# ScalarE's activation tables in a two-layer kernel: one load after every function, or a load where the written order needs one

## The chip, the cores and the metric

The kernel runs on one core of a Trainium2 chip. The metric is the device time of one execution in microseconds (us). A core has five engines that run beside each other and wait for one another by semaphores: TensorE (PE in the profile; its weight loads are PEld), VectorE (DVE), ScalarE (ACT), GpSimd (POOL) and SyncE (SP), which here only issues DMA transfers. All data is float32.

## The reference

The input x is two images of 48 x 48 positions with 768 channels. Two layers are applied, each as x + f(groupnorm(x)).

```python
# layer 0: attention of 12 heads, each position over the 7 x 7 positions around it
qkv = gn(x) @ w_qkv
scores = einsum('nhije,nhiajbe->nhijab', q * 64 ** -0.5, k_near)
o = einsum('nhijab,nhiajbe->nhije', softmax(scores), v_near)
x = x + o @ w_out
# layer 1: a selective scan over the 2304 positions, forwards and backwards, 1536 channels
xz = einsum('bld,ed->bel', gn(x), in_proj_w)
def branch(x, z):                       # once as it stands, once reversed, own parameters
    x = silu(dwconv(x, conv_w, conv_b))           # 4 taps
    dt, Bm, Cm = split(einsum('bdl,ed->bel', x, x_proj_w))
    delta = softplus(dt_proj_w @ dt + dt_proj_b)
    h = exp(delta * A) * h + (delta * x) * Bm     # for each of 16 states, along l
    y = sum over states of h * Cm, + x * Dp
    return y * silu(z)
x = x + einsum('bdl,cd->blc', forward + backward, out_proj_w)
```

Four functions need a table of ScalarE: exp (in softmax and in the scan), ln (in the group norm), silu and softplus.

## The kernel before, in words

**Tiling.** Positions lie along the free dimension in chunks of 384 (`CHUNKS`, six per image), channels on the 128 partitions in 12 blocks. Attention works on six row bands per image. The scan stage runs over units: image, direction, chunk, channel block, 2 x 2 x 6 x 12 = 288 units in this order. The states of a channel block are taken in four groups of four.

**One unit of the scan** (`scan`). For each group g: the input product hb = (delta x) * B, 128 x 1544 (L1225), on DVE from the PSUM tile `du` or on POOL from the tile `u`; ACT writes exp(delta A) for one state at a time, 128 x 384, into the PSUM tiles `da0` and `da1` (L1247), two states in each; DVE scans two states at once (L1258, `tensor_tensor_scan`) in place in `hb`; POOL multiplies by C (L1273); PE adds the 16 states up by transposes into `py` (L1290); ACT copies `py` to `yt` (L1316). ACT also copies `u` to `du` (L1202), the chunk's borders into `bc` (L1231) and the last state to `state` (L1281).

**Every third unit** (`deltas_of`). PE makes the pre-activation of delta for three channel blocks (L1151), ACT copies it into `dlt` (L1157) and takes softplus of 128 x 1152 at once (L1162), then ACT makes x * Dp (`vt`, L1170) and POOL makes delta x (L1175). That is 96 softplus.

**Beside the scan** (`in_proj`). For the next chunks PE makes x and z (L382), ACT does the convolution's first tap from PSUM into `uz` (L928), DVE the three others (L935), ACT copies z (L955), and `finish` takes silu (L961) of a whole `uz` tile, 128 x 2304, and stores it. The first chunk of image 0 goes before any scan: there six tiles of 128 x 1536 (named bc0 to bc7, borrowed buffers) are made, each followed by silu. That is 74 silu in all. Attention of image 1, the projections to delta, B and C (`x_proj`) and the output projections also run beside the scan.

**What sets the order.** All work is registered with `add`: an engine, an estimated duration in ns, a function that issues the instructions, and a key that says when it is wanted. `Order.run` (L153) then plays the program through with these estimates and writes out one order for all engines; each engine executes its instructions in this order. For each engine it picks among the works that are ready the one of smallest rank:

```python
over = max(0.0, t + x.ns - soon - self.DUE) / 2
rank = (max(t + over, free[e] + 150.0), x.first)
```

`t` is when the work could start, `soon` the earliest time at which a work marked `due` (the scan's exps) could start, DUE is 100 ns, and `over` counts only for works ahead of the oldest main key. Some input products have an `alt`: the planner may put them on DVE or on POOL. Where it sees TensorE idle long, it adds filler transposes (L1491).

**Tables.** The table that has exp and ln is loaded at the start (L263). The compiler places a load in front of each silu and softplus, and the kernel itself issues a load back directly after each (L962, L1163). The planner's estimate for both functions includes 2600 ns for the two loads.

Of the kernel before, what the change touches and what calls it, by code (L numbers as in the profile page):

```python
# [45 lines left out]
KB = 3  # L46
EARLY = 20
# [40 lines left out]
class Work:  # L88


    __slots__ = ("eng", "ns", "fn", "key", "job", "bufs", "waits", "then", "ready", "tail", "size", "first", "alt", "due", "opens")


class Order:
# [19 lines left out]
            for p in (parts,) if isinstance(parts, int) else parts:  # L114
                yield buf, p

    def add(self, eng, ns, fn, key, r=(), w=(), job=False, size=0, after=None, early=0, alt=None, due=False, opens=None):
        x = Work()
        x.eng, x.ns, x.fn, x.key, x.job, x.size = eng, ns, fn, key, job, size
        x.then, x.ready, x.tail, x.first = [], 0.0, self.TAIL[eng], key - early  # L120

        x.alt = alt

        x.due = due

        x.opens = opens
        before, bufs = set(), {}
        for buf, p in self.cells(r):
            c = (buf, p)
            bufs[buf] = None  # L130
            if c in self.wrote:
                before.add(self.wrote[c])
            self.read.setdefault(c, []).append(x)
        for buf, p in self.cells(w):
            c = (buf, p)
            bufs[buf] = None
            if c in self.wrote:
                before.add(self.wrote[c])
            before.update(self.read.pop(c, ()))
            self.wrote[c] = x  # L140
        before.discard(x)
        if after is not None:
            before.add(after)
        x.waits = len(before)
        for y in before:
            y.then.append(x)
        x.bufs = [b for b in bufs if b.pool is not None]
        for b in x.bufs:
            b.left += 1
        self.works.append(x)  # L150
        return x

    def run(self):  # L153
        free = dict.fromkeys(self.TAIL, 0.0)
        ready = {e: [] for e in free}
        slots, dma = {}, 0.0
        mains = sorted((x.key for x in self.works if not x.job), reverse=True)
        done_keys = {}
        for x in self.works:
            if not x.waits:  # L160
                ready[x.eng].append(x)
                assert not x.alt
        out = []
        left = len(self.works)
        extra, spare = 0.0, False
        while left:
            while mains and done_keys.get(mains[-1], 0):
                done_keys[mains[-1]] -= 1
                mains.pop()
            horizon = (mains[-1] if mains else 1e9) + self.LOOK + extra  # L170
            best = None
            for e, works in ready.items():
                pick = None
                soon = min((max(free[e], x.ready) for x in works if x.due), default=1e12)
                for x in works:
                    if x.key > horizon:
                        continue
                    t, more = max(free[e], x.ready), {}
                    for b in x.bufs:
                        if not b.end:  # L180
                            had = slots.get((b.pool, b.tag), ())
                            n = more[b.tag] = more.get(b.tag, 0) + 1
                            if len(had) + n > b.bufs:
                                old = had[n - 1 - b.bufs]
                                if old.left:
                                    t = None
                                    break
                                t = max(t, old.end + self.SEM)
                    if t is None:
                        continue  # L190
                    over = 0.0
                    if mains and x.key > mains[-1] < self.last and not x.due:
                        over = max(0.0, t + x.ns - soon - self.DUE) / 2
                    rank = (max(t + over, free[e] + 150.0), x.first)
                    if pick is None or rank < pick[0]:
                        pick = rank, t, x
                if pick and (best is None or pick[1] < best[0]):
                    best = pick[1], pick[2], e
            if not best:

                extra += 1.0
                assert extra < 400, "the plan is stuck"
                continue
            extra = 0.0
            t, x, e = best
            ready[x.eng].remove(x)
            gap = t - free["PE"]
            if e == "PE" and spare and gap > self.GAP:
                y = Work()
                y.eng, y.ns, y.key, y.job, y.size = e, 0.8 * (gap - 300.0), x.key, True, 0  # L210
                y.then, y.bufs, y.due, y.fn = [], [], False, lambda y=y: self.idle(y.ns)
                out.append((free[e], y))
            if x.opens is not None:
                spare = x.opens
            if x.alt:
                ready[x.alt[0]].remove(x)
                if e != x.eng:
                    x.eng, x.ns = x.alt
            for b in x.bufs:
                if not b.end:  # L220
                    slots.setdefault((b.pool, b.tag), []).append(b)
            free[x.eng] = t + x.ns
            if x.eng == "SP":
                dma = max(dma, t + 500.0) + x.size / 290.0
                end = max(dma, t + x.ns) + 2100.0
            else:
                end = t + x.ns + x.tail
            for b in x.bufs:
                b.left -= 1
                b.end = max(b.end, end)  # L230
            for y in x.then:
                y.waits -= 1
                y.ready = max(y.ready, end + self.SEM * (y.eng != x.eng))
                if not y.waits:
                    ready[y.eng].append(y)
                    if y.alt:
                        ready[y.alt[0]].append(y)
            if not x.job:
                done_keys[x.key] = done_keys.get(x.key, 0) + 1
            out.append((t, x))  # L240
            left -= 1
        return out
# [3 lines left out]
def tile_kernel(  # L246
# [3 lines left out]
    nc = tc.nc  # L250
# [74 lines left out]
    order = Order()  # L325
    marks = {"n": 0}
    pars = []

    def add(eng, ns, fn, key, r=(), w=(), job=False, size=0, after=None, early=0, alt=None, due=False, opens=None):

        news = [x[0] if isinstance(x, tuple) else x for x in w]

        def issue():
            for v in news:
                if v.ap is None:
                    v.ap = v.pool.tile(v.shape, F32, tag=v.tag, name=v.name, bufs=v.bufs)
            fn()

        if eng == "PE":

            ns *= 1.04 if key < 0 else 1.05
        return order.add(eng, ns, issue, key, r, w, job, size, after, early, alt, due, opens)

    def mm(n, cl):
        return n * (cl * 1.69 + 5)
# [1 line left out]
    def act(n, pointers=0):  # L347
        return 60 + 90 * pointers + n * 0.833
# [45 lines left out]
    def parameters(key):  # L394

        for i, (conv_w, conv_b, xpT, dtT, dt_b, A_log, Dp) in enumerate((fwd, bwd)):
# [15 lines left out]

            v = Buf(f"par{i}", ap=True)
            add("SP", 5000, fetch, key + i, w=[v], job=True)
            add("ACT", 800, decay, key + i + 0.5, r=[v], w=[v], job=True)
            pars.append(v)
        for j, t in enumerate(xd[0] + xd[1]):

# [8 lines left out]
    def group_norm(stats, n, key, job):  # L427
# [62 lines left out]
        for i, (eng, ns, fn, r, w) in enumerate((  # L490
# [10 lines left out]
            ("PE", 600, spread, [g, gT], [acc]),  # L501
            ("DVE", 200, last, [acc, mean], [rstd, shift]),
        )):
            add(eng, ns, fn, key + 0.01 * i, r, w, job=job)
        return shift, rstd

    def stats_of(b, key, job, tags):
# [21 lines left out]
    def attention(b, start, end, job, T):  # L529
# [228 lines left out]
        def heads(n, p, i, u, kc, ks, qs, vs, vat, mask, to, key):  # L758
# [16 lines left out]
            for j in range(2):  # L775
# [8 lines left out]
                def exponentials(j=j):  # L784
# [5 lines left out]
                add("DVE", dve(NKEY), masked, key, r=[sc[j], mask], w=[pr[j], (sm, j)], **S)  # L790
                add(
                    "ACT", act(NKEY, 1) + 90, exponentials, key, r=[pr[j], (sm, j)],
                    w=[pr[j], (sm, 2 + j)], **S,
                )

                if j or not job:
# [83 lines left out]
    def in_proj(b, i, start, end, conv=True, gate=True, nk=KB, tags=("uz",), banks=("mm",), proj=None):  # L880
# [78 lines left out]
        def finish(k0, nk, uz, dsts, key):  # L959
            def silu():  # L960
                nc.scalar.activation(uz[:, :, :, :cl], uz[:, :, :, :cl], AF.Silu)  # L961
                nc.scalar.preload_act_table_set("natural_log_exp_and_others")  # L962

            add("ACT", 2600 + act(len(dsts) * nk * cl), silu, key, r=[uz], w=[uz], job=True)
            for s, dst in enumerate(dsts):
                add(
                    "SP", 400,
# [160 lines left out]
    def deltas_of(ch, k0, x):  # L1128
# [31 lines left out]

        def softplus():
            nc.scalar.activation(dl[:, :, c], dl[:, :, c], AF.Softplus)  # L1162
            nc.scalar.preload_act_table_set("natural_log_exp_and_others")  # L1163

        add("ACT", 2600 + 120 + act(KB * cl), softplus, at + 0.05, [dl], [dl], early=EARLY)
        vts = [sb("vt", [P, CL], f"{n}_{j}") for j in range(KB)]
        for j in range(KB):
            add(
# [11 lines left out]
    def scan(ch, k, x, dlj, duj, vt):  # L1180
# [30 lines left out]
        def group(g):  # L1211
# [30 lines left out]
            def step(j):  # L1242
# [4 lines left out]
                    lambda: nc.scalar.activation(  # L1247
                        cells(da, 2)[:, j % 2, h], dl[:, jd, c], AF.Exp, scale=q["A"][:, k, i : i + 1]
                    ),
                    now + 0.06 * j - 0.06, [dlj], [(da, j % 2)], due=True,  # L1250
                )

            def two_steps(j):
# [242 lines left out]
    order.idle = idle  # L1496
    order.last = len(units) - 20
    with tc.manual_schedule():
        for _, x in order.run():
            x.fn()  # L1500


# [39 lines left out]
```

## Time and profile before

| | |
|---|---|
| runs, median (lowest to highest of 3) | 7051.39 us (7047.35 to 7055.09) |
| the profiled execution, its own time | 7056.32 us |
| its span, first to last instruction | 7054.5 us |
| mean granted clock of TensorE | 0.975 |
| instructions | 105645 |
| first scan | 1056.7 us after the span's start |
| DVE busy up to 1058 us / from there to the end | 423 us / 5638 of 5996 us |

The profile was taken from one execution; its durations belong to that execution, so a sum is made against 7056.32 us. A page of it lists busy time by engine, the span in 40 slices, the chain of work that ended last (followed back from the last instruction to what released it), and groups of equal instructions: line, engine, operation, what is written and read, count, then busy time in us and the mean in ns, then how long the engine sat idle just before them and for whom. The list of waits has, for each pair, the total in us, the number of times and the longest. In a timeline each line has start, duration, engine, line, operation, and in brackets the idle time before it. L1247 is line 1247 of the kernel before.

### The profile page before, as it was taken

The numbers are of one execution on the slowest core, as the hardware profiler recorded it, in microseconds if no ns is written. First come the engines' busy times: TensorE is split into PE (matmuls) and PEld (weight loads), VectorE is DVE, ScalarE is ACT, GpSimd is POOL, SyncE is SP. The second block draws the span as 40 slices with busy tenths as digits, with TensorE's granted clock in tenths as the row PEclk, the third lists the DMA queues.
The fourth block names the chain that finished last, engine by engine and source line by source line (L and its number), as shares of the span: only waits on it lengthen the run. The fifth ranks groups of instructions, "written<-read, shape, count | busy, mean of one in ns | idle before, by whom it ended". The sixth has DMA issues, their size and how long they took to land.

```text
span 7054.5 us, 105645 instructions
## 1 busy us (share of the span) xinstructions
PE 6334.5 (90%) x38151; PEld 4844.6 (69%) x38151; DVE 6061.2 (86%) x6217; ACT 4970.2 (70%) x10948; POOL 5447.5 (77%) x1951
## 2 busy tenths in 40 slices
PE   7999989999989998999988888888888898999888
PEld 5666656666667776676666656666678887777777
DVE  2354449999999999998898999999999999999998
ACT  1333248788887788887888778788876667777765
POOL 0000008888989999988898878999999999999997
PEclk9999989999999999999999999999999999999999
DMA  6565454444556444555444354343466676655553
GB/s 190 172 200 172 139 161 131 134 144 151 157 160 191 151 149 141 152 170 150 126 144 131 113 166 127 107 143 108 140 179 191 174 220 199 191 177 158 162 169 105
DMA packets 1337698, 1101.32 MB, mean 156 GB/s; under 512 B 136328, under 2 KB 1327416, under 8 KB 1337144
## 3 DMA queue, kind: packets, MB, share of 16 engines
q1 hardware_dynamic: 1337176, 1094.56, 52.1%
q8 instruction: 303, 4.96, 0.3%
q14 instruction: 219, 1.79, 0.1%
HBM read 881.41 MB, written 213.57 MB: 155 GB/s over the span
## 4 chain that ended last, share of the span: by engine, by line
DVE 39%; PE 19%; ACT 14%; POOL 12%; issue 9%; DMA 6%; SPq 1%; DVEq 0%; POOLq 0%; ACTq 0%
DVE hb L1258 25%; POOL hb L1273 8%; DVE hb L1225 7%; ACT da L1247 4%; PE mm_qk L382 4%; DVE uz_u L935 4%; POOL hb L1225 3%; PE py L1290 2%; PE mm_ao L382 2%; PE mm_v L382 2%; PE mm_xin L382 2%; ACT uz_u L928 1%; PE da L825 1%; ACT pr L785 1%; ACT L1163 1%
## 5 line engine op out<-in xcount | busy, mean ns | idle before, releaser
L1258 DVE TENSOR_TENSOR_SCAN hb<-da,hb 128x772 f32<-128x772 f32 x2304 | 3924.9, 1746 | 187.3 <-ACT da L1247 155.1
L1273 POOL TENSOR_TENSOR hb<-hb,bc 128x1536 f32<-128x1536 f32 x1152 | 3653.7, 3186 | 381.0 <-DVE hb L1258 338.3
L1247 ACT ACTIVATE da<-dlt,A 128x384 f32<-128x384 f32 x4608 | 2677.2, 584 | 915.2 <-DVE hb L1258 845.8
L1290 PE MATMUL py<-ident,hb 128*128 128x128 f32 x13824 | 1754.3, 279 | 264.3 <-POOL hb L1273 255.2
L1290 PEld LDWEIGHTS py<-ident,hb 128*128 128x128 f32 x13824 | 1570.9, 143 | 523.5 <-POOL hb L1273 413.6
L1225 POOL TENSOR_TENSOR hb<-u,bc 128x1544 f32<-128x1544 f32 x495 | 1584.6, 3203 | 22.6 <-PE py L1290 14.9
L1225 DVE TENSOR_TENSOR hb<-du,bc 128x1544 f32<-128x1544 f32 x657 | 1141.4, 1743 | 34.3 <-ACT du L1202 24.8
L1175 POOL TENSOR_TENSOR u<-dlt,u 128x384 f32<-128x384 f32 x288 | 263.8, 918 | 532.7 <-DMA bc<-xdf 412.6
L382 PE MATMUL mm_xin<-xc,w_x 128*128 128x390 f32 x1656 | 593.3, 504 | 25.3 <-DVE uz_u L935 16.2
L382 PE MATMUL mm_z<-xc,w_z 128*128 128x384 f32 x1728 | 608.1, 492 | 7.8 <-ACT dlt L1157 4.9
L382 PE MATMUL mm_out<-stage_y,w_o 128*128 128x192 f32 x3168 | 560.7, 332 | 18.1 <-ACT dlt L1157 6.4
L1491 PE MATMUL py<-ident 128*128 128x128 f32 x4431 | 550.4, 277 | 0.0
L382 PEld LDWEIGHTS mm_out<-stage_y,w_o 128*128 128x128 f32 x3168 | 522.0, 194 | 29.3 <-ACT dlt L1157 10.6
L1491 PEld LDWEIGHTS py<-ident 128*128 128x128 f32 x4431 | 503.3, 143 | 28.9 <-issue 26.0
L901 POOL MEMSET xc<- 128x18 f32 x4 | 0.5, 116 | 637.2 <-DVE sm L779 637.2
L382 PEld LDWEIGHTS mm_xin<-xc,w_x 128*128 128x128 f32 x1656 | 311.3, 195 | 238.3 <-issue 36.7
L935 DVE SCALAR_TENSOR_TENSOR uz_u<-mm_xin,conv_w,uz_u 128x384 f32<-128x384 f32 x792 | 428.3, 607 | 52.0 <-ACT uz_u L928 49.4
L382 PE MATMUL mm_qk<-xc_xn,w_qk 128*128 128x384 f32 x1296 | 459.1, 500 | 14.7 <-DMA w_qk<-in_w_qkv 3.1
L382 PEld LDWEIGHTS mm_z<-xc,w_z 128*128 128x128 f32 x1728 | 314.3, 192 | 194.4 <-issue 8.9
L382 PEld LDWEIGHTS mm_qk<-xc_xn,w_qk 128*128 128x128 f32 x1296 | 240.2, 194 | 173.8 <-issue 19.5
L785 ACT ACTIVATE pr<-pr,sm 128x308 f32<-128x308 f32 x432 | 234.5, 544 | 127.5 <-DVE sm L779 127.2
L1306 PE MATMUL py<-ident,vt 128*128 128x128 f32 x864 | 156.3, 292 | 146.3 <-ACT yt L1316 145.9
(163 smaller groups left out, 6780.9 us busy)
## 6 DMA issues: line engine op xcount, KB each, us to landing
w_o<-in_w_opT SPq DMA_DIRECT2D x264, 384.0 KB
bc<-xdf SPq DMA_DIRECT2D x96, 768.0 KB
bc<-xdb SPq DMA_DIRECT2D x96, 768.0 KB
w_qk<-in_w_qkv SPq DMA_DIRECT2D x144, 384.0 KB
w_x<-in_w_inT SPq DMA_DIRECT2D x144, 384.0 KB
w_z<-in_w_inT SPq DMA_DIRECT2D x144, 384.0 KB
w_ao<-in_w_out SPq DMA_DIRECT2D x72, 384.0 KB
u<-uf SPq DMA_DIRECT2D x48, 576.0 KB
```

The source lines that it names most:

```text
L382: nc.tensor.matmul(acc[:m, o0 : o0 + cl], wb[:, wi, wo : wo + m], xb[:, xi, xo : xo + cl], start=c == 0, stop=c == n - 1,)
L785: nc.scalar.activation(pr[j].ap, pr[j].ap, AF.Exp, bias=sm[:, j : j + 1], scale=-1.0, accum_out=sm[:, 2 + j : 3 + j],)
L825: nc.tensor.transpose(bank(pt, 512 - P)[:nk, k * P : (k + 1) * P], pr[j][:, c0 : c0 + nk], ident,)
L935: nc.vector.scalar_tensor_tensor(u, px[:, at[j] : at[j] + cl], q["conv_w"][:, k, j : j + 1], u, ALU.mult, ALU.add,)
L1175: lambda j=j: nc.gpsimd.tensor_mul(u[:, j, h], dl[:, j, c], u[:, j, h]), at + 0.06 + 0.25 * j,
L1225: on.tensor_mul(cells(hb, SG), by.unsqueeze(1).to_broadcast([P, SG, W]), bc[g].ap)
L1247: lambda: nc.scalar.activation(cells(da, 2)[:, j % 2, h], dl[:, jd, c], AF.Exp, scale=q["A"][:, k, i : i + 1]),
L1258: lambda: nc.vector.tensor_tensor_scan(flip(hb[at2]), flip(da[:, : 2 * W]), flip(hb[at2]), 0.0, ALU.mult, ALU.add),
L1273: lambda: nc.gpsimd.tensor_mul(cells(hb, SG)[:, :, h], cells(hb, SG)[:, :, h], bc[NSG + g][:, :, c]),
L1290: nc.tensor.matmul(py[:tp, t * P : (t + 1) * P], cells(hb, SG)[:, j, h][:, tb[t]], ident, start=False, stop=g == NSG - 1 and j == SG - 1 a ...
L1306: nc.tensor.matmul(py[:tp, t * P : (t + 1) * P], vt[:, tb[t]], ident, start=t == 0, stop=False, is_transpose=True, skip_group_check=True,)
L1491: nc.tensor.matmul(marks["py"][:, CL : CL + P], ident, ident, start=False, stop=False, is_transpose=True, skip_group_check=True,)
```

## The change

Each work now names its table (`table="exp"`, `"silu"`, `"softplus"` or none). The planner keeps the table that is loaded at that point of the order: when it has picked a work that needs another one, it adds 1294 ns to this work's duration. The fixed 2600 ns leave the estimates of silu and softplus. In the rank, while the table is not exp's, a work that needs silu's or softplus's table has 20 taken from its second part, which decides between equal first parts. When the order is issued, the load back to exp's table is written directly in front of the first work that needs it, no longer behind each silu and softplus.

```diff
-        extra, spare = 0.0, False
+        extra, spare, table = 0.0, False, "exp"
...
-                    rank = (max(t + over, free[e] + 150.0), x.first)
+                    own = x.table not in (None, "exp") and table != "exp"
+                    rank = (max(t + over, free[e] + 150.0), x.first - 20 * own)
...
+            if x.table and x.table != table:
+                x.ns += 1294.0
+                table = x.table
...
-            add("ACT", 800, decay, key + i + 0.5, r=[v], w=[v], job=True)
+            add("ACT", 800, decay, key + i + 0.5, r=[v], w=[v], job=True, table="exp")
...
-            add(eng, ns, fn, key + 0.01 * i, r, w, job=job)
+            add(eng, ns, fn, key + 0.01 * i, r, w, job=job, table="exp" if fn is root else None)
...
-                    w=[pr[j], (sm, 2 + j)], **S,
+                    w=[pr[j], (sm, 2 + j)], table="exp", **S,
...
                 nc.scalar.activation(uz[:, :, :, :cl], uz[:, :, :, :cl], AF.Silu)
-                nc.scalar.preload_act_table_set("natural_log_exp_and_others")
-
-            add("ACT", 2600 + act(len(dsts) * nk * cl), silu, key, r=[uz], w=[uz], job=True)
+            add(
+                "ACT", act(len(dsts) * nk * cl), silu, key, r=[uz], w=[uz], job=True, table="silu",
+            )
...
             nc.scalar.activation(dl[:, :, c], dl[:, :, c], AF.Softplus)
-            nc.scalar.preload_act_table_set("natural_log_exp_and_others")
-
-        add("ACT", 2600 + 120 + act(KB * cl), softplus, at + 0.05, [dl], [dl], early=EARLY)
+        add("ACT", 120 + act(KB * cl), softplus, at + 0.05, [dl], [dl], early=EARLY, table="softplus")
...
-                    now + 0.06 * j - 0.06, [dlj], [(da, j % 2)], due=True,
+                    now + 0.06 * j - 0.06, [dlj], [(da, j % 2)], due=True, table="exp",
...
     with tc.manual_schedule():
+        table = "exp"
         for _, x in order.run():
+            if x.table == "exp" != table:
+                nc.scalar.preload_act_table_set("natural_log_exp_and_others")
+            table = x.table or table
             x.fn()
```

More of the change, by code (lines that the diff above doesn't have):

```diff
@@ L88 @@
 class Work:
-    __slots__ = ("eng", "ns", "fn", "key", "job", "bufs", "waits", "then", "ready", "tail", "size", "first", "alt", "due", "opens")
+    __slots__ = ("eng", "ns", "fn", "key", "job", "bufs", "waits", "then", "ready", "tail", "size", "first", "alt", "due", "opens", "table")
 class Order:
@@ L115, in cells, with add @@
                 yield buf, p
-    def add(self, eng, ns, fn, key, r=(), w=(), job=False, size=0, after=None, early=0, alt=None, due=False, opens=None):
+    def add(self, eng, ns, fn, key, r=(), w=(), job=False, size=0, after=None, early=0, alt=None, due=False, opens=None, table=None):
         x = Work()
@@ L126, in add @@
         x.opens = opens
+        x.table = table
         before, bufs = set(), {}
@@ L210, in run @@
                 y.eng, y.ns, y.key, y.job, y.size = e, 0.8 * (gap - 300.0), x.key, True, 0
+                y.table = None
                 y.then, y.bufs, y.due, y.fn = [], [], False, lambda y=y: self.idle(y.ns)
@@ L327, in tile_kernel, with add @@
     pars = []
-    def add(eng, ns, fn, key, r=(), w=(), job=False, size=0, after=None, early=0, alt=None, due=False, opens=None):
+    def add(eng, ns, fn, key, r=(), w=(), job=False, size=0, after=None, early=0, alt=None, due=False, opens=None, table=None):
         news = [x[0] if isinstance(x, tuple) else x for x in w]
@@ L341, in add @@
             ns *= 1.04 if key < 0 else 1.05
-        return order.add(eng, ns, issue, key, r, w, job, size, after, early, alt, due, opens)
+        return order.add(eng, ns, issue, key, r, w, job, size, after, early, alt, due, opens, table)
     def mm(n, cl):
```

## The prediction

> **What bounds the kernel now.** I read the page first: busy time by engine, then the chain of work that ended last.
>
> ```profile
> PE 6334.5 (90%) x38151; PEld 4844.6 (69%) x38151; DVE 6061.2 (86%) x6217; ACT 4970.2 (70%) x10948; POOL 5447.5 (77%) x1951
> DVE 39%; PE 19%; ACT 14%; POOL 12%; issue 9%; DMA 6%; SPq 1%; DVEq 0%; POOLq 0%; ACTq 0%
> DVE hb L1258 25%; POOL hb L1273 8%; DVE hb L1225 7%; ACT da L1247 4%; PE mm_qk L382 4%; DVE uz_u L935 4%; POOL hb L1225 3%; PE py L1290 2%; PE mm_ao L382 2%; PE mm_v L382 2%; PE mm_xin L382 2%; ACT uz_u L928 1%; PE da L825 1%; ACT pr L785 1%; ACT L1163 1%
> ```
>
> The shares mix two stages. Busy time in 40 stretches shows VectorE (DVE) at 423 us in the first 1058 us (image 0's attention, TensorE at work) and at 5638 of the remaining 5996 us, the scan stage: 94%, 358 us idle. GpSimd (POOL) is at 91% there. So DVE sets the pace and its idle time is what can be won or lost. ScalarE (ACT) matters where it makes DVE wait. The groups of ACT's instructions give the loads:
>
> ```profile
> L1162 ACT ACT_TABLE_LOAD x96 | 123.2, 1283 | 1.5
> L1163 ACT ACT_TABLE_LOAD x96 | 123.2, 1283 | 1.6
> ...
> L961 ACT ACT_TABLE_LOAD x74 | 94.9, 1283 | 1.3
> L962 ACT ACT_TABLE_LOAD x74 | 94.9, 1283 | 1.3
> ```
>
> 340 loads of 1283 ns are 436 us of ACT: one ahead of each softplus (L1162) and silu (L961), one back to exp's table after it (L1163, L962). Summed over the pieces of the chain, 142 of them lie on it, 176 us. Who waits for ACT is in DVE's waits of the scan stage, 1058 to 7054 us:
>
> ```profile
> DVE hb L1258 <- ACT da L1247: 155.1, 116, 6.3
> DVE uz_u L935 <- ACT uz_u L928: 37.6, 36, 3.9
> ...
> DVE hb L1225 <- ACT du L1202: 16.3, 22, 1.7
> ```
>
> How a load becomes such a wait stands in the timeline of ACT around one softplus, and DVE's line after it:
>
> ```profile
> 2409.60 1.20 ACT L1247 ACTIVATE da<-dlt,A 128x384 f32<-128x384 f32 x2 [0.45 <-DVE hb L1258]
> 2410.82 1.28 ACT L1162 ACT_TABLE_LOAD   x1
> 2412.11 1.16 ACT L1162 ACTIVATE dlt<-dlt 128x1152 f32<-128x1152 f32 x1
> 2413.30 1.28 ACT L1163 ACT_TABLE_LOAD   x1
> ...
> 2415.45 1.21 ACT L1247 ACTIVATE da<-dlt,A 128x384 f32<-128x384 f32 x2
> ```
>
> ```profile
> 2416.68 3.42 DVE L1258 TENSOR_TENSOR_SCAN hb<-da,hb 128x772 f32<-128x772 f32 x2 [2.14 <-ACT da L1247]
> ```
>
> The two da tiles let exps run two scans ahead, about 3.5 us (a scan is 1746 ns). The block load, softplus, load takes 3.76 us, copies follow, and DVE stands for 2.14 us.
>
> **What the Trainium skill says.** "ScalarE: Activation LUTs", section What ACT_TABLE_LOAD costs, gives about 1283 ns for a load and 1380 ns of drain, 2.66 us a switch. The trace agrees on 1283 and shows no drain: 1.283 + 1.166 + 1.283 = 3.73 of the block's 3.76 us. I price a switch at 1.283. Its section Table sets: the hidden batching unit says that cheap functions (copy, identity) are in every set; so copies and the convolution's first tap (L928) can run under silu's or softplus's table. The trace of before doesn't show that, as none runs there.
>
> **The change part by part.** The order of both programs can be compared, since a planner writes it out at build time.
>
> *Loads.* 340 become 326: 96 before softplus, 69 before silu, 161 back to exp. 11 of the 14 that go are in one place, the head (six silus of image 0's first chunk, 977 to 1030 us, no exp between them); 3 in the rest. Up to the first silu ACT's orders are the same.
>
> *Head.* The chain of before there has these pieces (start, us, what):
>
> ```profile
> 1002.09 1.28 ACT L962
> ...
> 1024.59 1.28 ACT L961
> ...
> 1027.38 1.28 ACT L962
> ```
>
> They are 3.85 us of chain; the head's other loads lie beside DVE's or TensorE's work there and are hidden. Without them the silu of 1025.88 still waits for DVE's taps, but these begin earlier, because ACT's first tap at 1020.83 no longer follows a load. 3 to 6 us: I take -4.
>
> *The 3 other loads*: 3 x 1.283 = 3.8 us of ACT x 0.40 (176/436, the share of load time on the chain) = -1.5.
>
> *DVE or POOL.* The planner puts 8 of the input products (hb<-du, 1743 ns on DVE, 3203 on POOL) on POOL: -13.9 us of DVE, +25.6 of POOL. Weighted with the chain's share of each (481/1141 and 244/1585): -5.9 + 3.9 = -2. The 86 more filler transposes on PE (277 ns each, 24 us) are put in gaps of PE: nothing; if none were a gap, +24.
>
> *Where a softplus stands.* The planner picks for ACT by a rank in which a work that runs ahead is held back by half of what it delays the next due exp. For softplus the work counted was 3740 ns (2600 for loads, 1140 of its own); with the exp due d ns after ACT is free it won once (3740 - 100 - d)/2 <= d, d >= 1213. Now the pick counts 1140, and the 1294 of each load is added only after it: d >= 347. For silu 1493 becomes 626. So a block of unchanged length goes into thinner cover. I counted this off both orders with the durations of the rows: for each softplus, ACT's work from the exps of the scan before it to those of the scan after it, against DVE's work from the scan that releases the first of them to the scan that needs the last. Before: 7.86 us of ACT under 8.15 of DVE on average, 34 of 96 short, by 56.5 us in all. After: 8.16 under 7.68, 42 of 95 short, by 95.1. That is 38.5 us more. In the trace the scans behind softplus blocks waited 37.4 us where the count says 56.5, so the low end is 0.66 x 38.5 = +25; with the waits for du, pr and uz_u after the same blocks it was 57, so the high end is 1.0: +38.5. I take the high end, because exps are now drawn ahead of these copies (18 softplus have no other work before the next exp, 7 before). Silu blocks: short by 34.8 before, 31.4 after: -3. Scans without a table near them: 109 before, 78 after; but there the count hardly follows the trace's waits (correlation 0.27, for softplus 0.59). I take 0 and keep -31 as an end.
>
> *Reload behind the copies.* The load back now stands in front of the next exp instead of behind the function; copies between come 1.283 us sooner, exps do not. In before DVE waited for du and uz_u behind such reloads; each wait cut at 1.283 gives 14.3 + 3.1 + 9.3 + 5.6 = 32.3 us. Such works stand between function and exp 47 times in after, 71 in before: 32.3 x 47/71 = -21 at best, 0 at worst. I take -12. The other way round: a copy that waits for PE now holds the reload and the exp behind it; in before that wait hid the load. Up to 1.283 each; inside the range.
>
> Sum: -4 - 1.5 - 2 + 38.5 - 3 - 12 = +16 us on the profiled execution, 7056.3 (span 7054.5 and 1.8 around it): 7072. The median of the runs is 4.9 lower, so 7067. What is late next: a late scan delays POOL's output product (L1273, which waited 338 us for scans), then PE's summing and the hb buffer.
>
> **Rivals.** A run can tell 0.2%, 14 us, from no change.
>
> *Nothing to be told.* Thin cover at its low end and copies at their best: -4 - 1.5 - 2 + 25 - 3 - 21 = -6.5, about 7045; without copies +14.5. For it: ACT is at 70% and idles before exps for 915 us, and 96% of the loads stay. Against: 155 us of DVE already wait for exps.
>
> *Faster.* One mechanism, the reload that leaves the way of the copies. Place: the 170 functions; price: the full 32.3 us, where copies moved behind the exp gain too; it decides once the thin cover costs no more than 0.66 of its count: -4 - 1.5 - 2 + 25 - 3 - 32 = -17.5, 7034. For it: 40 of before's waits behind reloads, up to 3.9 us each, end with uz_u or du. Against: fewer of these works stand there now. With the -31 of the scans without tables it reaches 7003.
>
> *Much slower.* A planner's new order may lose elsewhere (POOL at 91%, weights that land later); no row of the profile prices it. I allow up to a seventh of DVE's 358 us of idle time once more, 50: 7117.
>
> **How the numbers follow.** Slower, the forecast, 0.43 (own range 7066 to 7120); no difference 0.29; faster 0.28. 7067 is the forecast's; the range 7015 to 7120 leaves 1 in 10 on each side.
>
> **What would show it.** In the profile after: 326 loads, one from 977 to 1030; the first scan (1056.7) 3 to 6 us earlier; input products at 649 on DVE and 503 on POOL; DVE's wait for da above 155 us, by about 25, mostly behind softplus; its waits for uz_u and du below 37.6 and 16.3. The prediction is wrong if da's wait doesn't grow, or if DVE's idle time moves for something else than ACT (PE, POOL, DMA) by more than 20 us.

## The result and the profile after

Over six runs of each, the changed kernel takes 7072.1 us in the median (7061.11 to 7078.08) against 7053.4 us (7047.35 to 7064.39) before: a ratio of 1.0021, 95% interval 1.0011 to 1.0031. It is slower by 0.2%. The profiled execution took 7078.1 us (span 7076.0), 21.8 us over the one before.

Busy time by engine and the chain of work that ended last, on the page of the changed kernel:

```profile
PE 6356.0 (90%) x38237; PEld 4861.8 (69%) x38237; DVE 6051.3 (86%) x6209; ACT 4950.4 (70%) x10934; POOL 5474.6 (77%) x1959
DVE 35%; PE 20%; ACT 17%; POOL 12%; issue 10%; DMA 6%; SPq 1%; DVEq 0%; POOLq 0%; ACTq 0%
DVE hb L1266 23%; POOL hb L1281 8%; DVE hb L1233 6%; ACT da L1255 5%; PE mm_qk L390 4%; POOL hb L1233 3%; DVE uz_u L943 3%; PE py L1298 3%; PE mm_ao L390 2%; PE mm_v L390 2%; ACT L1510 1%; DMA bc<-xdf 1%; PE mm_xin L390 1%; DMA bc<-xdb 1%; ACT pr L793 1%
```

ACT is busy for 20 us less than before and holds more of the chain: 17% for 14%. DVE did 10 us less and the kernel still grew, so DVE stood idle for longer. The groups of ACT's loads in the changed kernel (line, operation, count, busy us, mean ns, idle before):

```profile
L1510 ACT ACT_TABLE_LOAD x161 | 206.6, 1283 | 2.6
...
L1171 ACT ACT_TABLE_LOAD x96 | 123.2, 1283 | 1.5
...
L969 ACT ACT_TABLE_LOAD x69 | 88.5, 1283 | 1.2
```

That is 326 loads of unchanged length. L1510 is the load back to exp's table, in front of the exp. DVE's waits for ACT from 1060 us to the end (total us, times, longest us):

```profile
DVE hb L1266 <- ACT da L1255: 198.8, 134, 9.1
DVE hb L1233 <- ACT du L1210: 29.3, 18, 6.7
DVE uz_u L943 <- ACT uz_u L936: 28.9, 45, 3.2
```

The scans wait 199 us for exps where they waited 155, the input products 29 us for du where they waited 16, the taps 29 for 38. From the first scan to the last instruction DVE is idle for 387 us (before: 352), gaps of a few tens of ns left out. I sorted this idle time by the function that ended less than 7 us earlier: behind softplus 104 us for 66, behind silu 90 for 77, elsewhere 193 for 209. So most of the loss stands behind softplus, and some behind silu. Against 10 us less DVE work these 35 us make the scan stage 24.4 us longer (6022.3 for 5997.9), and the first scan starts 3.0 us earlier (1053.7 for 1056.7): 21.4 of the span's 21.5 us.

One softplus of the changed kernel, on ACT, then DVE's scans beside it:

```profile
3912.80 1.28 ACT L1171 ACT_TABLE_LOAD   x1
3914.10 1.17 ACT L1171 ACTIVATE dlt<-dlt 128x1152 f32<-128x1152 f32 x1
3915.28 1.28 ACT L1510 ACT_TABLE_LOAD   x1
3916.58 2.32 ACT L1255 ACTIVATE da<-dlt,A 128x384 f32<-128x384 f32 x4
```

```profile
3913.21 1.75 DVE L1266 TENSOR_TENSOR_SCAN hb<-da,hb 128x772 f32<-128x772 f32 x1
3917.88 1.77 DVE L1266 TENSOR_TENSOR_SCAN hb<-da,hb 128x772 f32<-128x772 f32 x1 [2.92 <-ACT da L1255]
```

When the block begins, DVE has one scan left for which the exps are there; then it stands for 2.92 us.

### The profile page after: what moved, and what is told of

The parts are those of the page before. It is cut to its first block, busy times and chain, and to the rows that moved or that the text cites. A ratio compares the mean times of both kernels' runs of the same rounds, so it can differ in the third digit from the quotient of the medians.

```text
span 7076.0 us, 105794 instructions
## 1 busy us (share of the span) xinstructions
PE 6356.0 (90%) x38237; PEld 4861.8 (69%) x38237; DVE 6051.3 (86%) x6209; ACT 4950.4 (70%) x10934; POOL 5474.6 (77%) x1959
## 4 chain that ended last, share of the span: by engine, by line
DVE 35%; PE 20%; ACT 17%; POOL 12%; issue 10%; DMA 6%; SPq 1%; DVEq 0%; POOLq 0%; ACTq 0%
DVE hb L1266 23%; POOL hb L1281 8%; DVE hb L1233 6%; ACT da L1255 5%; PE mm_qk L390 4%; POOL hb L1233 3%; DVE uz_u L943 3%; PE py L1298 3%; PE mm_ao L390 2%; PE mm_v L390 2%; ACT L1510 1%; DMA bc<-xdf 1%; PE mm_xin L390 1%; DMA bc<-xdb 1%; ACT pr L793 1%
## 5 line engine op out<-in xcount | busy, mean ns | idle before, releaser
L1233 POOL TENSOR_TENSOR hb<-u,bc 128x1544 f32<-128x1544 f32 x503 | 1611.2, 3205 | 16.0 <-PE py L1298 8.7
L1233 DVE TENSOR_TENSOR hb<-du,bc 128x1544 f32<-128x1544 f32 x649 | 1126.3, 1744 | 49.5 <-ACT du L1210 36.6
L1160 PE MATMUL mm_dl<-dt,dtw 49*128 49x384 f32 x576 | 252.9, 541 | 44.1 <-ACT dlt L1166 13.3
```

The lines of the kernel that those rows point to most:

```text
L1160: lambda j=j, acc=acc: nc.tensor.matmul(acc[:, c], w[:, j * P : (j + 1) * P], dt[:, c], start=True, stop=True),
L1233: on.tensor_mul(cells(hb, SG), by.unsqueeze(1).to_broadcast([P, SG, W]), bc[g].ap)
```

## The experiments

The change has two parts that can be set apart: which order the planner writes (the pick without the loads, and the charge of 1294 ns at the function and at the next exp), and where the load back is issued in that order. One part can be settled without a run: the order that comes out without the 20 taken from the rank is the same program, instruction by instruction. "Works of one kind of table go together" did nothing here. The 14 loads fewer don't come from the planner either: the order of before has 326 loads too, if each is issued only where the next function needs another table.

Every kernel below computes the whole reference; ratios are to the kernel before on the same chip.

**Only the place of the load, on the order of before** (lazy_only).

```diff
     with tc.manual_schedule():
         for _, x in order.run():              # planner, estimates and order as before
+            if x.table == "exp" != table:
+                nc.scalar.preload_act_table_set("natural_log_exp_and_others")
+            table = x.table or table
             x.fn()
             # and no preload behind silu and softplus
```

> The planner and so the order of all engines are those of the kernel before; only the load back to exp's table is issued directly in front of the next work that needs it (326 loads instead of 340). Theory (the written order is what loses, the later load by itself gains): the first scan 3 us earlier, waits for uz_u and du behind silu and softplus cut, together 54 us before, to 35 to 45; the wait for da stays at 155 +-10; time 10 to 20 us below before, ratio 0.997 to 0.9986. Rival (the later load itself harms, because a copy that waits now holds the load and the exp behind it): da's wait grows by 15 us or more, ratio 1.001 or above. Rival (nothing: ScalarE is not the bound): ratio within 0.999 to 1.001.

Measured: ratio 1.0044 (1.0031 to 1.0056), slower by 31 us with 14 loads fewer and the same order. The theory I had stated fell; the first rival holds. DVE's waits from 1060 us in this run:

```profile
DVE hb L1264 <- ACT da L1253: 202.6, 140, 7.8
DVE uz_u L941 <- ACT uz_u L934: 33.0, 39, 3.7
DVE hb L1231 <- ACT du L1208: 6.5, 12, 1.3
```

The waits for the copies fell, as forecast: du 6.5 us for 16.3, uz_u 33.0 for 37.6. That uz_u's fall comes from the place of the load is not shown: it is as large in the next run (31.1), where the load stays behind the function. The exps lost 47 us. One silu shows why. ACT's timeline of the kernel before:

```profile
1498.67 1.28 ACT L962 ACT_TABLE_LOAD   x1
1500.14 0.20 ACT L1231 COPY bc<-state 128x8 f32<-128x8 f32 x1 [0.18 <-POOL hb L1225]
1500.24 0.47 ACT L955 COPY uz_z<-mm_z 128x384 f32<-128x384 f32 x1
1501.51 0.20 ACT L1231 COPY bc<-state 128x8 f32<-128x8 f32 x1 [0.80 <-DVE hb L1225]
1501.61 0.19 ACT L1281 COPY state<-hb 128x4 f32<-128x4 f32 x1
1501.71 1.70 ACT L1247 ACTIVATE da<-dlt,A 128x384 f32<-128x384 f32 x3
```

And the same silu with the load in front of the exp, then DVE's line that waits for it:

```profile
1497.58 2.13 ACT L967 ACTIVATE uz_u<-uz_u 128x2304 f32<-128x2304 f32 x1 [0.63 <-DVE uz_u L941]
1501.40 0.20 ACT L1237 COPY bc<-state 128x8 f32<-128x8 f32 x1 [1.69 <-POOL hb L1231]
1501.50 0.47 ACT L961 COPY uz_z<-mm_z 128x384 f32<-128x384 f32 x1
1502.57 0.20 ACT L1237 COPY bc<-state 128x8 f32<-128x8 f32 x1 [0.59 <-DVE hb L1231]
1502.67 0.19 ACT L1287 COPY state<-hb 128x4 f32<-128x4 f32 x1
1502.87 1.28 ACT L1508 ACT_TABLE_LOAD   x1
1504.16 1.71 ACT L1253 ACTIVATE da<-dlt,A 128x384 f32<-128x384 f32 x3
```

```profile
1505.40 3.42 DVE L1264 TENSOR_TENSOR_SCAN hb<-da,hb 128x772 f32<-128x772 f32 x2 [1.20 <-ACT da L1253]
```

The bc copy behind the silu can't start until POOL has read the old bc. Before, the load ran in that time; the load waits for nothing. Now ACT idles 1.69 us at the copy, and the load is paid after it. Added up from the functions to the next exps of the scan stage, ACT idles 54 us ahead of such loads (0 before), and the way from the end of a function to the next exp takes 400 us in all for 359.

**The same 14 loads left out, the others back behind the function** (elide_before).

```diff
+        for x in works:                       # the order of before
+            x.fn()
+            if x.table in ("silu", "softplus") and after[x] == "exp":   # the next table in the order
+                nc.scalar.preload_act_table_set("natural_log_exp_and_others")
```

> The order of the kernel before on all engines. The 14 loads that need not be there are left out (326 loads), but each load back stays directly behind the last silu or softplus ahead of an exp. It differs from the run with the load in front of the exp only in the place of the loads. Theory (there the load stands in ScalarE's queue behind copies that wait, 54 us of idle time ahead of loads): the first scan about 3 us earlier, no idle time ahead of loads, da's wait 150 to 165 us, ratio 0.998 to 1.0005. Rival (the leaving out of loads itself upsets the order): ratio 1.002 or above.

Measured: 0.9988 (0.9981 to 0.9994), 10 us faster. Its scans' waits for exps:

```profile
DVE hb L1264 <- ACT da L1253: 149.5, 112, 6.3
```

ACT idles 0 us ahead of loads. The first scan comes 7.2 us earlier than before, where 3 were expected. The two runs have the same order, the same instructions and the same 326 loads and by their ratios stand 40 us apart, so the place of the load is the cause.

**The order of the changed kernel with the load behind the function** (after_eager).

```diff
                 nc.scalar.activation(uz[:, :, :, :cl], uz[:, :, :, :cl], AF.Silu)
+                nc.scalar.preload_act_table_set("natural_log_exp_and_others")
...
             nc.scalar.activation(dl[:, :, c], dl[:, :, c], AF.Softplus)
+            nc.scalar.preload_act_table_set("natural_log_exp_and_others")
...
-            if x.table == "exp" != table:
-                nc.scalar.preload_act_table_set("natural_log_exp_and_others")
-            table = x.table or table
```

> The order of the changed kernel on all engines, but with the load back directly behind each silu and softplus as before (340 loads). Theory (the written order is what loses): slower than the changed kernel by what the later load gains, 10 to 20 us, so 30 to 45 us over before, ratio 1.0042 to 1.0065; da's wait at or above 199. Rival (the later load harms): faster than the changed kernel, ratio to before below 1.001, da's wait below 185.

Measured: 1.0067 (1.0053 to 1.0081), slower than the changed kernel's 1.0021. On this order the load in front of the exp gains, by 0.46%, 28 us between the medians; on the order of before it lost 31. Both figures include the 14 loads left out, which alone gave 10 us on the order of before; what they give on this order was not run. The order was written with a charge for the load at the exp, and in the scan stage it has fewer works between a function and the next exp: 345, where the order of before has 535. ACT idles only 12 us ahead of loads in the changed kernel. That the charge is what makes the difference is argued, not shown. The gain is above the 10 to 20 us expected, and da's wait, 191 us, is below the 199. That the sign depends on the order is not something my theory had said.

**Only the pick, on the kernel before** (pick_light).

```diff
-                        over = max(0.0, t + x.ns - soon - self.DUE) / 2
+                        over = max(0.0, t + x.ns - 2600 * (x.table in ("silu", "softplus")) - soon - self.DUE) / 2
```

> The kernel before with one change in the planner: in the pick the loads' 2600 ns are not counted (the hold-back of softplus and silu sees 1140 and 1979 ns); the charge stays 2600 at the function and the load back directly behind it. Theory as in the prediction (the lighter pick puts softplus into thinner cover): da's wait behind softplus from 34 to 50 or more, ratio 1.002 to 1.005. Rival (the lighter pick alone does little; the count on this order gives softplus short by 62 us in all where before gives 56 and the changed kernel 95, and silu by 22 for 35): da's wait behind softplus 34 to 42, ratio 0.998 to 1.0015.

Measured: 1.0097 (1.0083 to 1.0111), slower by 68 us. Behind softplus the scans' waits for exps go from 34 to 58 us, those for du from 8 to 24, for uz_u from 3 to 13. In total, from 1060 us:

```profile
DVE hb L1266 <- ACT da L1255: 184.9, 142, 5.5
DVE hb L1233 <- ACT du L1210: 42.0, 33, 4.5
DVE uz_u L941 <- ACT uz_u L934: 36.1, 30, 3.8
```

The mechanism holds, and its size, expected up to 1.005, was too small: DVE's idle time behind softplus grows by 49 us, and DVE is also busy for 12 us longer. The count of short softplus on this order, 62 us for 56, had suggested next to nothing; it looks only at exps, and at one scan.

**The pick put back in the changed kernel** (after_pick_heavy), and then for one function alone (heavy_softplus, heavy_silu).

```diff
-                        over = max(0.0, t + x.ns - soon - self.DUE) / 2
+                        over = max(0.0, t + x.ns + 2600 * (x.table in ("silu", "softplus")) - soon - self.DUE) / 2
# heavy_softplus: 2600 for "softplus" alone; heavy_silu: for "silu" alone
```

> The changed kernel with one change in the planner: in the pick softplus and silu count 2600 ns more, as before. The charge stays 1294 at the function and 1294 at the next exp. Theory as in the prediction: the cover comes back, da's wait behind softplus falls from 61 to 35 to 45, time 20 to 30 us below the changed kernel, ratio to before 0.997 to 0.9995. Rival (the split charge is what loses, the exp picked without its load): da's wait behind softplus stays above 50, ratio 1.001 to 1.004.

> The changed kernel; in the pick only softplus counts 2600 ns more (as before the change), silu stays light. Theory (softplus in thin cover is what the lighter pick costs): most of the 45 us between the changed kernel and the one with both held back comes back, ratio to before 0.995 to 0.998, da's wait behind softplus 25 to 35 us. Rival (silu's pick matters as much): half of it, ratio 0.998 to 1.0005.

> The changed kernel; in the pick only silu counts 2600 ns more, softplus stays light. The count on this order gives softplus short by 100 us (the changed kernel 95, both held back 59). Theory (softplus): as slow as the changed kernel or slower, ratio 1.001 to 1.005, da's wait behind softplus 50 us or more. Rival (silu's pick matters as much): ratio 0.998 to 1.0005.

Measured: both held back 0.9956 (0.9944 to 0.9969), softplus alone 0.9961 (0.9949 to 0.9974), silu alone 1.0043 (1.0029 to 1.0056). The waits of the first, after_pick_heavy:

```profile
DVE hb L1266 <- ACT da L1255: 157.7, 121, 7.7
DVE uz_u L943 <- ACT uz_u L936: 27.9, 33, 3.1
DVE hb L1233 <- ACT du L1210: 15.7, 18, 2.2
```

Against the changed kernel, the scans' waits behind softplus fall from 61 to 25 us and all waits for du from 29 to 16. With softplus alone they are 29 and 19; with silu alone 58 and 35. So the lighter pick of both costs 0.65% of the time (0.9956 to 1.0021, some 45 us), more than the 20 to 30 expected. Softplus's makes up nearly all of it, and of silu's nothing is to be seen. Two of these kernels beat both the kernel before and the changed one, by 0.4 and 0.6%.

**The held-back order with the load behind the function** (heavy_eager): after_pick_heavy with the edit of after_eager.

> The order of the kernel with both held back (0.9956), but with the load back directly behind each silu and softplus (340 loads). Theory (the later load gains where the planner has charged it to the exp): slower than the same order with the later load by 20 to 35 us, as between the changed kernel and its order with the early load (28 us), so ratio to before 0.9985 to 1.0005. Rival (an order by which ScalarE is held back gains whatever the place of the load): ratio 0.995 to 0.9975.

Measured: 1.0035 (1.0021 to 1.0048). The direction is as expected, the size nearly twice it: 0.79% by the ratios, 49 us by the medians against before, with 17 loads more than the held-back kernel has. All of the gain of the held-back order goes with the load in front of the exp. Here the loss is at the copies, from 1060 us:

```profile
DVE uz_u L943 <- ACT uz_u L936: 56.6, 41, 4.4
DVE hb L1235 <- ACT du L1212: 29.2, 26, 4.8
```

That is 57 us for 28 at uz_u and 29 for 16 at du, while the exps wait less (143 us for 158): copies behind a function now wait for a load that they don't need.

Taken together: where the planner charged both loads to the function, the load behind it is faster (0.9988 against 1.0044). Where it charged one to the exp, the load in front of the exp is (1.0021 against 1.0067, 0.9956 against 1.0035). Issue and charge gain when they agree. That rests on three orders; the light pick with both loads charged to the function and the load in front of the exp was not run.

**Neighbours**, to see how far a new order by the same rules moves the time: the charge 1283 instead of 1294 ns, with the held-back pick (heavy_1283) and with the light one (light_1283).

```diff
-                x.ns += 1294.0
+                x.ns += 1283.0
```

> The changed kernel with softplus and silu held back by 2600 ns in the pick, and the charge of a load 1283 ns instead of 1294: a neighbour that changes no rule and makes another order, to see how far an order drawn anew moves the time. Theory (the hold-back decides): within 15 us of the one with 1294, ratio 0.9935 to 0.998, da's wait behind softplus 25 to 40 us. Rival (the gain of the first was the luck of one order): anywhere from 0.998 to 1.004.

> The changed kernel with the charge of a load 1283 ns instead of 1294: a neighbour of the changed kernel, light pick, another order. The count gives softplus short by 67 us (the changed kernel 95, its held-back neighbours 56 and 59) and scans without a table near by 126 (78, 85, 89). Theory (the light pick decides): slower than its held-back neighbour (0.998) by 20 us or more, ratio 1.001 to 1.006. Rival (orders drawn anew spread as far as the pick moves the time): 0.9995 or below.

Measured: 0.998 (0.9974 to 0.9987) and 1.0088 (1.0074 to 1.0102). The rule's sign stays: held back against light is 0.9956 against 1.0021 in one pair, 0.998 against 1.0088 in the other. But a neighbour lies 0.24% away with the held-back pick, 17 us where at most 15 were expected, and 0.67% with the light one, above the range of 1.001 to 1.006. The changed kernel is the better of the two light orders.

What repeats better than the time is DVE's idle time behind softplus. In the three pairs with a heavy and a light pick it moves by 49 us (before and pick_light), 42 (both held back and the changed kernel) and 48 (the two with 1283). The times move by 68, 45 and 76.

The granted clock of TensorE differs between the runs too. Among executions of one kernel the longer ones show the lower clock: in elide_before 7065.9 us at 0.972 and 7033.6 at 0.980, and over the executions of all kernels some 3.6 us go with 0.001. The means of the kernels lie between 0.974 (pick_light, lazy_only) and 0.980 (heavy_softplus); the kernel before and the changed one both have 0.976. Brought to one clock with this slope, an estimate, the light pick costs about 60, 34 and 80 us in the three pairs, and the place of the load moves the time by about 30 (lazy_only against elide_before), 27 (after_eager against the changed kernel) and 40 (heavy_eager against both held back). The held-back kernel stays ahead of before by 18 us instead of 30. No sign turns, but a part of these sizes goes with the clock; whether the order is what moves the clock is open.

## Why the prediction was right

Forecast were 16 us on the profiled execution and a median of 7067; measured were 21.8 and 7072.1. Step by step:

- **Loads.** 326, as counted, of which one lies from 977 to 1030 us. That the planner groups nothing was open to me: I read 14 loads fewer as part of the change's order, and they belong to the issuing alone.
- **Head, -4.** Right. From the first normalized block of the chunk to the first scan it takes 96.3 us before and 91.8 after, -4.5; in the other profiles 90.7 to 93.6 with 3 loads there, 96.8 to 96.9 with 14. Of the start of the scans itself only 3.0 us show, since the stage ahead of it, whose order doesn't change, moves by some us from one execution to the next.
- **The 3 other loads, -1.5.** Not seen by itself. All 14 together, the head's 11 included, gave 10 us with nothing else changed (elide_before).
- **DVE or POOL, -2.** The counts are right (649 and 503), DVE's busy time fell by 9.9 us. Its share in the end was not measured.
- **Thin cover of softplus, +38.5.** The mechanism is shown, from both sides: taking the loads out of the pick alone made the kernel before 68 us slower, putting them back made the changed one 45 us faster. In the profile DVE's idle time behind softplus grew by 38 us. The term was nevertheless mis-sized: it held exps alone (measured +27 behind softplus), and the light pick also makes the input products wait for du (29 us for 16 with both picks held back). Its price in time is 45 to 76 us in three pairs of kernels, of which 42 to 49 are DVE's idle time behind softplus; the rest comes from elsewhere in the new orders.
- **Silu, -3.** Wrong in sign: the scans' waits for exps behind silu went from 45 to 59 us. Holding silu back in the pick does not take them away (61 in heavy_silu), so the pick is not their cause. lazy_only on the order of before shows the same rise (67), so the load that waits behind copies can make it; but with the load behind the function the changed order still has 58. What makes it there stays open.
- **Reload behind the copies, -12.** Half right. uz_u's waits fell by 8.7 us. du's rose by 13, against the sign that I had given; the pick explains it. On the changed order the later load does gain: 28 us with the 14 loads left out, so perhaps 18 without these (an estimate, from the 10 us of elide_before), half as much again as my term. What I had put at "inside the range", a copy that waits and holds the load and the exp, is a cost of its own: on the order of before it outweighs the gain of the copies, 40 us between two runs that differ in nothing but the place of the load.

So the sum was right because its losses and its gains were both too small by about as much: the pick costs 45 us or more where 38.5 stood, and issue and charge together give 31 us (0.9956 with the held-back pick) where 4 + 1.5 + 2 + 3 + 12 = 22.5 stood. And a neighbour of the changed kernel under the same rules lies 45 us higher; that the result fell within 5 us of the forecast is in part the luck of the order that was drawn.

Of the rivals, "faster" named the right mechanism: with softplus held back it decides, and the kernel is 0.4% faster than before. The condition that I gave for it, a thin cover at its low price, was not met in the changed kernel.

## What to carry to other kernels

When a planner's estimate is made truer, look at every place that reads it: here the fixed 2600 ns was a charge and at the same time what held a long work back from a thin spot, and only the charge was replaced. An instruction without a wait, such as a table load, belongs ahead of those that may wait in the same queue, if the order leaves idle time there; in front of its user it is paid in full whenever the work between them has to wait. Behind works that are ready and that another engine waits for, it is better placed later, as the held-back order shows. So take an edit apart into the order and the place in the order, and run each on the other's ground: here the later load gained 0.5 and 0.8% on two orders and lost 0.4% on a third.

## What the runs showed of the hardware

Copies and the convolution's first tap run under silu's and softplus's tables without a load: between function and next exp the changed kernel has no loads but the one back, 326 in all. The table load starts while the engine's next activation still waits: in the kernel before one starts at 1494.62 us and takes 1.28, and the silu behind it begins at 1496.53, after 0.63 us of waiting for DVE. A load, a softplus and a load take 3.76 us, 1.283 + 1.166 + 1.283 and 0.03 between them. The 1380 ns of drain that the prediction quotes do not show: in all twelve profiles ACT stands idle for at most 0.02 us before a load, the first of the program apart, and for as little after it where the next instruction waits for no semaphore.
